# A gather-and-sum graph layer: x rows transposed on TensorE, 66 single rows per step, and steps of the start and the end moved

## The chip, the cores and the metric

The kernel runs on one core of a Trainium2 chip. The metric is the device time of one execution in microseconds; the median of several executions counts.

## The reference

One layer of a graph network with 50,000 nodes of 128 float32 features and 1,650,000 edges, sorted by destination. Each node has an edge to itself.

```
Xs   = x[src]
msg  = where(edge_type == 0, Xs @ W_data.T + b_data, Xs @ W_control.T + b_control)
agg  = segment_sum(msg, dst)
h    = x + relu(agg + x @ W_self.T + b_self)
out  = (h - mean(h)) / sqrt(var(h) + 1e-5)          # per node
```

## The kernel before, in words

The kernel first sums rows of x per destination and per edge type, and multiplies by the weights after that. Edges are cut into blocks that follow each other in the sorted list. A block has Q = 2 steps; a step has R = 12 chunks of 128 edges, F = 42 edges whose rows are found in another way, and S = 64 single edges. So a block covers BE = 24 x 128 + 2 x 42 + 2 x 64 = 3284 edges (lines 35 to 45). There are NBLK = 503 blocks. The first and the last are "plain": chunks only. The last has RCH = 13 chunks.

**Gathers (line 464).** For every chunk GpSimd (POOL) issues one indirect DMA that brings 128 rows of x into a buffer. Six chunks are a pass; a block has four passes; there are SLOTS = 10 buffers of one pass each. TensorE (PE) waits for a pass with a semaphore (line 471), and then multiplies each chunk of rows with a one-hot matrix of 128 x 120 (line 483), which sums the rows by destination (60 columns) and type (two halves).

**Single rows (lines 428 to 443).** For the S single edges of a step, each row of x is loaded with a DMA of its own, half by SP and half by the scalar engine (ACT). Before the DMAs of a step, each of the two loads the byte offsets of its 32 rows from SBUF into registers with one instruction (line 435). The rows are for the block AHEAD = 2 blocks later. PE waits for them at line 449 and adds them with the product of line 489. The offsets are computed by the vector engine (DVE) in `offsets` (line 426).

**The F edges.** DVE finds which of the block's edges to the node itself, for which the node's own row is at hand, can be replaced by these edges, and puts new indices into the gather's list (`fill`, lines 300 to 330), five blocks ahead. What was left out is added back from the transposed rows xT (line 361).

**The window of a block (lines 386 to 396).** A block's sums lie in a window of B = 112 nodes. SP loads the window's first node from SBUF into a register, one block at a time (line 387), then loads the rows of x twice: as they are (xw, 112 x 128, line 393) and transposed (xT, 128 x 112, line 395, from a transposed copy of x in device memory). This is three blocks ahead.

**The layer (lines 514 to 543).** PE adds xT with the self weights, the biases and the two sums with their weights in a PSUM tile po (lines 517, 518, 520). DVE makes h = max(po, 0) + xw (line 525), then the moments (527, 529); ACT takes the root (534); DVE scales (540, 542); SP stores the rows (543).

**The order of the work** is written out by hand in the loop at line 566 for each block and pass, and each engine's queue keeps it. At the head of a block stand the window of block b + 3, then the last sums of the block before; behind the first pass the layer and the moments of the block before, the one-hot matrix for block b + 2 and the single rows of its first step; behind the second pass the root and the counts; behind the third the store, `fill` for b + 5 and the single rows of the second step; behind the fourth the offsets for b + 3.

**The start.** The weights are loaded into two buffers that are freed afterwards and transposed by PE (lines 904 to 911). SP's first load is the index list of block 0 (line 116). POOL makes the number row num (line 120) and the matrix below (133); DVE copies num to PSUM (127).

**The end.** When all blocks are done, DVE and PE work out a flag that tells whether the input breaks an assumption (lines 615 to 640). All engines load the flag (line 919), and branch over a general version that is used only if it is set.

Of the kernel before, what the change touches and what calls it, by code (L numbers as in the profile page):

```python
# [11 lines left out]
F32 = mybir.dt.float32  # L12
# [10 lines left out]
N = 50000  # L23
# [11 lines left out]
W = 60  # L35
# [2 lines left out]
B = 112  # L38
C = R * Q
F = 42  # L40
S = 64
X = Q * S
R1 = R + 1
C1 = Q * R1
# [40 lines left out]
def straight(ctx, tc, c, x, x_t, src_t, dst_t, etype_t, src_f, dst_f, etype_f, src_x, dst_first, first_p, out):  # L85
# [38 lines left out]
    num_ps, rank_no_ps = small[:, :2 * W], small[:, 2 * W:2 * W + F]  # L124
    lists = [small[:, 2 * W + F + i * FILL:][:, :FILL] for i in range(2)]
    sums_at = [small[:Q * F, 2 * W + F + 2 * FILL + i:][:, :1] for i in range(2)]
    nc.vector.tensor_copy(num_ps, num)

    ones_b = keep.tile([P, P], BF16, name="ones_b")
    nc.vector.memset(ones_b, 1.0)  # L130
# [1 line left out]
    below = keep.tile([P, P], BF16, name="below")  # L132
    nc.gpsimd.affine_select(out=below, in_=ones_b, pattern=[[1, P]], compare_op=ALU.is_gt, fill=0.0,
                            base=0, channel_multiplier=-1)
    rank_no = keep.tile([P, F], F32, name="rank_no")
    nc.vector.tensor_scalar(rank_no, num[:, :F], -LOOP, None, op0=ALU.add)
    nc.vector.tensor_copy(rank_no_ps, rank_no)
# [243 lines left out]

    idxs = {0: idx0}
    bys, pcs, zs, pls, bases, ats, ys = {}, {}, {}, {}, {}, {}, {}
    ohs, cnts, accs, xws, xTs, pos, hs, mvs, sds = {}, {}, {}, {}, {}, {}, {}, {}, {}

    def base_of(b):
        return nc.values_load(base_i[0:1, b:b + 1], engines=[SP], min_val=0, max_val=N - B,
                              skip_runtime_bounds_check_because="it was clamped to this")

    def window(b):  # L390
        at = bases[b] = base_of(b)
        xw = stp.tile([B, D], F32, name="xw", bufs=5)
        nc.sync.dma_start(xw, x[bass.ds(at, B), :])
        xT = stp.tile([P, B], F32, name="xT", bufs=5)
        nc.sync.dma_start(xT, x_t[:, bass.ds(at, B)])
        xws[b], xTs[b] = xw, xT

    def onehot(b):
        g, i = divmod(b, GB)
# [13 lines left out]

    ROW_SLOTS = AHEAD + 2
    TURN = S // 2
    LOAD = TURN // 1
    RANGE = dict(min_val=0, max_val=(N - 1) * ROW, skip_runtime_bounds_check_because="where a node's row is")
    x_bytes = x.rearrange("n d -> (n d)").bitcast(U8)[None, :]
    fetched = [[tc.alloc_semaphore(f"fetched{j}_{i}") for i in range(ROW_SLOTS)] for j in range(2)]
# [8 lines left out]
    def single_rows(b, q, part):  # L428

        if q == 0 and part == 0:  # L430
            ys[b] = stp.tile([S, Q, D], F32, name="yx", bufs=ROW_SLOTS)
        both = []
        for j, (eng, dma) in enumerate(((SP, nc.sync), (ACT, nc.scalar))):
            at = j * TURN + part * LOAD
            _, rows = nc.values_load_multi_w_load_instructions(
                ats[b][0:1, q * S + at:q * S + at + LOAD], engines=[eng], **RANGE)
            both.append([(dma, fetched[j][b % ROW_SLOTS], at + k, row) for k, row in enumerate(rows)])
        for pair in zip(*both):
            for dma, sem, k, row in pair:
                copy = dma.dma_start(ys[b][k:k + 1, q, :].bitcast(U8), x_bytes[:, bass.ds(row, ROW)])  # L440
                copy.then_inc(sem, 16)
                tc.no_tile_sem_insts.add(copy.ins.name)
                tc.add_to_no_dep_group(f"single{b}", copy.ins)
# [69 lines left out]

    def layer(b):
        a = sums[b % RING]
        po = ps_o.tile([B, D], F32, name="po")
        nc.tensor.matmul(po, xTs.pop(b), c["wselfT"], start=True, stop=False)  # L517
        nc.tensor.matmul(po, a[0:3, 2, :B], bias, start=False, stop=False)  # L518
        for t in range(2):
            nc.tensor.matmul(po, a[:, t, :B], c["wmsgT"][:, t * D:(t + 1) * D], start=False, stop=t == 1)  # L520
        pos[b] = po

    def moments(b):
        h = stp.tile([B, D], F32, name="h")
        nc.vector.scalar_tensor_tensor(h, pos.pop(b), 0.0, xws.pop(b), op0=ALU.max, op1=ALU.add)  # L525
        st = stp.tile([B, 6], F32, name="st")
        nc.vector.bn_stats(st, h)  # L527
        mv = stp.tile([B, 2], F32, name="mv")
        nc.vector.bn_aggr(mv, st)
        hs[b], mvs[b] = h, mv  # L530
# [6 lines left out]
    def store(b):  # L537
# [4 lines left out]
        nc.vector.tensor_scalar(o, hs.pop(b), mv[:, 0:1], rstd, op0=ALU.subtract, op1=ALU.mult)  # L542
        nc.sync.dma_start(out[bass.ds(bases.pop(b), B), :], o)

    for b in range(1, AHEAD + 1):
        offsets(b)
    columns(0)
# [6 lines left out]
    for b in range(1, RAHEAD):  # L554
        fill(b)
        left_out_columns(b)
        left_out_matrix(b)
        if b < AHEAD:
            onehot(b)
            counts(b)  # L560
            for q in range(Q):
                for part in range(1):
                    single_rows(b, q, part)
        if b == 1:
            clear_sums()
    for b in range(NBLK + 1):
        if b + 3 < NBLK:
            window(b + 3)
        g, i = divmod(b, GB)
        if i == 0 and g + 1 < GROUPS:  # L570
            load_edges(g + 1)
        if i == 3 and g + 1 < GROUPS:
            spread_out(g + 1)
        if i == 4 and g + 1 < GROUPS:
            spread_in(g + 1)
        if b > 0:
            add(b - 1, steps_of(b - 1)[-1])
        if b < NBLK:
            begin_sums(b)
        last = steps_of(b)[-1:]  # L580
        for q, (step, ks) in enumerate(passes_of(b)):
            if ks:
                products(b, step, ks)
            if q == 0 and b > 0:
                layer(b - 1)
            if q == 1:
                left_out_numbers(b + 1)
            if q == 3:
                left_out_columns(b + RAHEAD)
            if ks and step not in last and ks[-1] == chunks_of(b, step)[-1]:  # L590
                add(b, step)
            if q == 0 and b > 0:
                moments(b - 1)
            if q == 0 and b + AHEAD < NBLK:
                onehot(b + AHEAD)
            if q == 1 and b > 0:
                root(b - 1)
            if q == 2 and b > 0:
                store(b - 1)
            if q == 1 and b + AHEAD < NBLK:  # L600
                counts(b + AHEAD)
            if q == 2 and i == 2 and g + 1 < GROUPS:
                columns(g + 1)
            if q == 2:
                left_out_rows(b + 1)
                if b + RAHEAD < NBLK:
                    fill(b + RAHEAD)
            if q == 3:
                left_out_matrix(b + RAHEAD)
                offsets(b + AHEAD + 1)  # L610
            if q % 2 == 0 and not plain(b + AHEAD):
                single_rows(b + AHEAD, q // 2, 0)


    ones = keep.tile([P, 1], F32, name="ones")
    nc.vector.memset(ones, 1.0)
    mm = keep.tile([P, 2], F32, name="mm")
    nc.vector.tensor_reduce(mm[:, 0:1], stats[:, :, 0, :], AX.XY, ALU.min)
    nc.vector.tensor_reduce(mm[:, 1:2], stats[:, :, 1, :], AX.XY, ALU.max)
    bad = keep.tile([P, 3], F32, name="bad")  # L620
    least = keep.tile([P, 1], F32, name="least")
    nc.vector.tensor_reduce(least, loops, AX.X, ALU.min)
    nc.vector.tensor_scalar(bad[:, 2:3], least, float(F), None, op0=ALU.is_lt)
    nc.vector.tensor_scalar(bad[:, 0:1], mm[:, 0:1], 0.0, None, op0=ALU.is_lt)
    nc.vector.tensor_scalar(bad[:, 1:2], mm[:, 1:2], float(W), None, op0=ALU.is_ge)
    gap = keep.tile([1, 3], F32, name="gap")
    nc.vector.tensor_reduce(gap[:, 0:1], shift, AX.X, ALU.min)
    nc.vector.tensor_reduce(gap[:, 1:2], shift, AX.X, ALU.max)
    nc.vector.tensor_scalar(gap[:, 0:1], gap[:, 0:1], 0.0, None, op0=ALU.is_lt)
    nc.vector.tensor_scalar(gap[:, 1:2], gap[:, 1:2], float(B), None, op0=ALU.is_gt)  # L630
    pb = ps_o.tile([B, D], F32, name="po")
    nc.tensor.matmul(pb[:3, 0:1], bad, ones, start=True, stop=True)
    both = keep.tile([3, 1], F32, name="both")
    nc.vector.tensor_copy(both, pb[:3, 0:1])
    pc = ps_o.tile([B, D], F32, name="po")
    nc.tensor.matmul(pc[:1, 0:1], both, ones[:3, 0:1], start=True, stop=True)
    nc.vector.tensor_copy(gap[:, 2:3], pc[:1, 0:1])
    total = keep.tile([1, 1], F32, name="total")
    nc.vector.tensor_reduce(total, gap, AX.X, ALU.add)
    nc.vector.tensor_copy(c["bad"], total)  # L640


def general(ctx, tc, c, x, src, dst, etype, out):
# [221 lines left out]
def gnn_resnorm(  # L865
# [35 lines left out]
    nc.vector.memset(eps, EPS)  # L901
    wmsgT = const.tile([P, 2 * D], F32, name="wmsgT")
    wselfT = const.tile([P, D], F32, name="wselfT")
    with tc.tile_pool(name="wts", bufs=2) as wts, \
            tc.tile_pool(name="wts_ps", bufs=2, space=bass.MemoryType.PSUM) as wts_ps:
        for w, o in ((w_data, wmsgT[:, :D]), (w_ctrl, wmsgT[:, D:]), (w_self, wselfT)):
            w_sb = wts.tile([P, D], F32, name="w_sb")
            nc.scalar.dma_start(w_sb, w)
            pw = wts_ps.tile([P, D], F32, name="pw")
            nc.tensor.transpose(pw, w_sb, ident)  # L910
            nc.scalar.copy(o, pw)
# [63 lines left out]
```

## Time and profile before

| | us |
|---|---|
| timed runs | 24035.24, 24102.25, 24134.87 |
| median | 24102.25 |
| profiled execution, its own time | 15118.55 |
| profiled execution, span | 15116.8 |
| mean granted TensorE clock in it | 0.544 |

The profiled execution is shorter than the timed runs by 8983.70 us. Durations and waits below come from it, since a trace exists for it alone. The page gives busy time and share for each engine, then the chain of work that ended last, then groups of instructions: line, engine, operation, the tiles written and read, the count, busy time and mean duration in ns, and behind the bar the idle time of the engine just before them and what ended it. An engine's name with a q is its queue: control, register loads and the issue of DMAs. "issue" is time in which the engine waited for nothing that the profile shows.

Its DMA queues moved 970.59 MB in 753,407 packets, at 64 GB/s; the 16 DMA engines were busy for 26.4% of the span. Two queues issue the single rows: 32,064 from SP and 32,064 from ACT.

### The profile page before, as it was taken

The page shows a single profiled execution, that of the slowest core. Times are in us where ns is not written, and L with a number is a line of the kernel's source. Part 1 is how long each engine was busy: PE and PEld are TensorE (multiplying, and loading weights), DVE is VectorE, ACT ScalarE, POOL GpSimd, SP SyncE. Part 2 cuts the span into 40 slices and gives each one's busy share as a digit, 9 for nine tenths or more (in the row PEclk, how much of TensorE's full clock was granted, in tenths as well). Part 3 has the DMA queues.
Part 4 walks back from the last instruction along what each step waited for, and adds up shares of the span by engine and source line. Part 5 has one row for each costly group of instructions (what it writes and reads, how often), then busy time and mean ns, then how long its engine had stood idle before and what let it go on. Part 6 is the DMA issues. An engine that isn't in the chain of part 4 may idle for free.

```text
span 15116.8 us, 243274 instructions
## 1 busy us (share of the span) xinstructions
PE 8042.1 (53%) x34836; PEld 6872.7 (45%) x34837; DVE 10626.1 (70%) x13316; ACT 151.7 (1%) x509; POOL 11399.7 (75%) x12071
## 2 busy tenths in 40 slices
PE   3555555555555555555555555555555555555555
PEld 3444444444444444444444444444444444444444
DVE  8776676767767767776676767767777676767765
ACT  0000000000000000000000000000000000000000
POOL 7777777777777777777777777777777777777777
PEclk7555555555555555555555555555555555555555
DMA  2332222222222222222222222222222222222222
GB/s 66 64 65 64 65 65 64 64 65 65 64 65 64 65 64 65 64 65 64 65 64 65 64 65 64 65 64 65 65 64 64 65 65 64 64 65 65 64 65 58
DMA packets 753407, 970.59 MB, mean 64 GB/s; under 512 B 355317, under 2 KB 552100, under 8 KB 751779
## 3 DMA queue, kind: packets, MB, share of 16 engines
q0 software_dynamic: 385968, 791.19, 21.5%
q1 hardware_dynamic: 301244, 146.99, 4.0%
q10 hardware_dynamic: 64566, 16.74, 0.6%
q14 instruction: 1345, 11.01, 0.2%
q8 instruction: 284, 4.65, 0.1%
HBM read 924.76 MB, written 29.02 MB: 63 GB/s over the span
## 4 chain that ended last, share of the span: by engine, by line
POOL 59%; issue 20%; PE 9%; DMA 6%; DVE 4%; ACTq 1%; SPq 0%; POOLq 0%; PEldq 0%; ACT 0%; PEld 0%; DVEq 0%
POOL y L464 59%; DMA y<-in_x,idx 6%; PE acc L483 6%; PE po L520 2%; PE po L518 1%; PE po L517 1%; ACTq L440 1%; DVE cnt L409 0%; DVE by L329 0%; DVE h L525 0%; DVE st L527 0%; DVE m L310 0%; DVE new L313 0%; DVE v_new L317 0%; DVE old L326 0%
## 5 line engine op out<-in xcount | busy, mean ns | idle before, releaser
L464 POOL DMA_INDIRECT y<-in_x,idx x12048 | 11385.9, 945 | 3683.0 <-issue 3573.7
L483 PE MATMUL acc<-oh,y 128*128 128x120 f32 x24122 | 5753.1, 428 | 6277.9 <-PEq L471 6263.0
L483 PEld LDWEIGHTS acc<-oh,y 128*128 128x128 f32 x24122 | 5208.8, 325 | 6688.2 <-PEq L471 6663.4
L409 DVE TENSOR_REDUCE cnt<-oh 128x240 bf16<-128x3120 f32 x503 | 2914.2, 5794 | 0.1
L525 DVE SCALAR_TENSOR_TENSOR h<-po,xw 112x128 f32<-112x128 f32 x503 | 146.7, 292 | 2994.7 <-PE po L520 2937.1
L401 DVE TENSOR_TENSOR oh<-col,small 128x3120 f32<-128x3120 f32 x503 | 1695.9, 3372 | 0.0
L329 DVE TENSOR_REDUCE by<-old 128x84 bf16<-128x1092 f32 x501 | 1066.7, 2129 | 17.4
L499 DVE TENSOR_TENSOR sums<-acc,sums 128x180 f32 x1006 | 347.2, 345 | 960.0 <-PE acc L492 900.9
L489 PE MATMUL acc<-oh,yx 64*128 64x120 f32 x2004 | 769.3, 485 | 7.4 <-PEq L449 7.4
L310 DVE TENSOR_TENSOR m<-rk,small 128x1092 f32<-128x1092 f32 x501 | 647.3, 1292 | 17.1
L313 DVE TENSOR_TENSOR new<-m,small 128x1092 f32<-128x1092 f32 x501 | 647.1, 1292 | 17.1
L317 DVE TENSOR_REDUCE v_new<-new 128x26 f32<-128x1092 f32 x501 | 646.8, 1291 | 17.1
L326 DVE TENSOR_TENSOR old<-m,small 128x1092 f32<-128x1092 f32 x501 | 643.2, 1284 | 0.0
L489 PEld LDWEIGHTS acc<-oh,yx 64*128 64x128 f32 x2004 | 492.5, 303 | 215.9 <-issue 204.6
L520 PE MATMUL po<-wmsgT,sums 128*112 128x128 f32 x2012 | 527.7, 408 | 0.0
L336 PE MATMUL small<-ones_b,by 128*84 128x1 bf16 x501 | 113.0, 225 | 733.2 <-DVE by L329 728.7
L520 PEld LDWEIGHTS po<-wmsgT,sums 128*112 128x112 f32 x2012 | 383.7, 262 | 111.9 <-issue 97.8
L336 PEld LDWEIGHTS <-by 128*84 128x84 bf16 x501 | 73.7, 147 | 791.0 <-DVE by L329 787.1
L518 PE MATMUL po<-bias,sums 3*112 3x128 f32 x1006 | 356.9, 452 | 0.2 <-DVE sums L499 0.2
L517 PE MATMUL po<-wselfT,xT 128*112 128x128 f32 x1006 | 316.9, 419 | 0.0
L512 DVE TENSOR_TENSOR sums<-pl,sums 128x336 f32<-128x336 f32 x501 | 254.3, 508 | 85.0 <-DVE sums L499 83.9
L534 ACT ACTIVATE sd<-mv,eps 112x1 f32<-112x1 f32 x503 | 148.3, 295 | 14831.2 <-PE acc L483 6098.9
(115 smaller groups left out, 3640.2 us busy)
## 6 DMA issues: line engine op xcount, KB each, us to landing
yx<-in_x ACTq DMA_DIRECT2D x32064, 0.5 KB
yx<-in_x SPq DMA_DIRECT2D x32064, 0.5 KB
y<-in_x,idx POOLq DMA_INDIRECT x12048
xw<-in_x SPq DMA_DIRECT2D x503, 56.0 KB
xT<-in_x_t SPq DMA_DIRECT2D x503, 56.0 KB
out<-o SPq DMA_DIRECT2D x503, 56.0 KB
vf_all<-vd SPq DMA_DIRECT2D x51, 420.0 KB
s<-in_src_t SPq DMA_DIRECT2D x51, 130.0 KB
```

Source lines behind the costliest of these rows:

```text
L310: nc.vector.tensor_tensor(m, rk_g[g][:, i, :, None].to_broadcast([P, C1, F]), rank_no_ps[:, None, :].to_broadcast([P, C1, F]), op=ALU.is_e ...
L313: nc.vector.tensor_tensor(new.rearrange("p (q r) f -> p q r f", r=R1), m.rearrange("p (q r) f -> p q r f", r=R1), vf.rearrange("p (q f) -> ...
L317: nc.vector.tensor_reduce(v, new, AX.X, ALU.add)
L326: nc.vector.tensor_tensor(old, m, cb[:, :, None].to_broadcast([P, C1, F]), op=ALU.mult)
L329: nc.vector.tensor_reduce(by, old.rearrange("p (q r) f -> p q f r", r=R1), AX.X, ALU.add)
L401: nc.vector.tensor_tensor(oh, col_g[g][:, i, :, None].to_broadcast([P, C1, 2 * W]), num_ps[:, None, :].to_broadcast([P, C1, 2 * W]), op=AL ...
L409: nc.vector.tensor_reduce(cnt, ohs[b].rearrange("p (q r) w -> p q w r", r=R1), AX.X, ALU.add)
L464: copy = nc.gpsimd.indirect_dma_start(out=y[:r, k % PASS, :], out_offset=None, in_=x, in_offset=bass.IndirectOffsetOnAxis(ap=idxs[b][:r, c ...
L483: nc.tensor.matmul(acc[:, :2, :].rearrange("p t w -> p (t w)"), y[:r, k % PASS, :], ohs[b][:r, column(k), :], start=k == of_step[0], stop= ...
L489: nc.tensor.matmul(acc[:, :2, :].rearrange("p t w -> p (t w)"), ys[b][:, q, :], ohs[b][:S, q * R1 + R, :], start=False, stop=True)
L518: nc.tensor.matmul(po, a[0:3, 2, :B], bias, start=False, stop=False)
L520: nc.tensor.matmul(po, a[:, t, :B], c["wmsgT"][:, t * D:(t + 1) * D], start=False, stop=t == 1)
```

## The change

- S goes from 64 to 66. A block covers 3288 edges, and there are 502 blocks; the last has 23 chunks, the last chunk 112 edges.
- The single rows of a step are loaded in two parts of 17 and 16 rows for each of SP and ACT, behind every pass instead of every other one. Each part has its own load of offsets.
- xw is no longer loaded. PE transposes xT into a second half of the PSUM tile po, DVE copies that to h, and then adds max(po, 0) to it.
- The bases of the windows are loaded for five blocks with one instruction.
- The weights have a buffer each, which is not freed. The copy of num to PSUM stands behind the making of below.
- The flag is worked out before the last block's gathers instead of after everything; its code is otherwise the same.

```
-S = 64
+S = 66
...
-    nc.vector.tensor_copy(num_ps, num)
...
     nc.gpsimd.affine_select(out=below, in_=ones_b, pattern=[[1, P]], compare_op=ALU.is_gt, fill=0.0,
                             base=0, channel_multiplier=-1)
+    nc.vector.tensor_copy(num_ps, num)
...
+    BASES = 5
     def window(b):
-        at = bases[b] = base_of(b)
-        xw = stp.tile([B, D], F32, name="xw", bufs=5)
-        nc.sync.dma_start(xw, x[bass.ds(at, B), :])
+        if b % BASES == 0:
+            n = min(BASES, NBLK - b)
+            _, regs = nc.values_load_multi_w_load_instructions(
+                base_i[0:1, b:b + n], engines=[SP], min_val=0, max_val=N - B,
+                skip_runtime_bounds_check_because="it was clamped to this")
+            bases.update({b + i: at for i, at in enumerate(regs)})
+        at = bases[b]
...
-    LOAD = TURN // 1
+    LOAD = -(-TURN // 2)
...
             at = j * TURN + part * LOAD
+            n = min(LOAD, (j + 1) * TURN - at)
             _, rows = nc.values_load_multi_w_load_instructions(
-                ats[b][0:1, q * S + at:q * S + at + LOAD], engines=[eng], **RANGE)
+                ats[b][0:1, q * S + at:q * S + at + n], engines=[eng], **RANGE)
...
     def layer(b):
         a = sums[b % RING]
-        po = ps_o.tile([B, D], F32, name="po")
-        nc.tensor.matmul(po, xTs.pop(b), c["wselfT"], start=True, stop=False)
+        both = ps_o.tile([B, 2, D], F32, name="po")
+        po, xT = both[:, 0, :], xTs.pop(b)
+        nc.tensor.transpose(both[:, 1, :], xT, c["ident"])
+        nc.tensor.matmul(po, xT, c["wselfT"], start=True, stop=False)
...
     def moments(b):
         h = stp.tile([B, D], F32, name="h")
-        nc.vector.scalar_tensor_tensor(h, pos.pop(b), 0.0, xws.pop(b), op0=ALU.max, op1=ALU.add)
+        po = pos.pop(b)
+        nc.vector.tensor_copy(h, po[:, 1, :])
+        nc.vector.scalar_tensor_tensor(h, po[:, 0, :], 0.0, h, op0=ALU.max, op1=ALU.add)
...
     for b in range(NBLK + 1):
+        if b == NBLK - 1:
+            find_bad()
...
-            if q % 2 == 0 and not plain(b + AHEAD):
-                single_rows(b + AHEAD, q // 2, 0)
+            if not plain(b + AHEAD):
+                single_rows(b + AHEAD, q // 2, q % 2)
...
-        for w, o in ((w_data, wmsgT[:, :D]), (w_ctrl, wmsgT[:, D:]), (w_self, wselfT)):
-            w_sb = wts.tile([P, D], F32, name="w_sb")
+        for i, (w, o) in enumerate(((w_data, wmsgT[:, :D]), (w_ctrl, wmsgT[:, D:]), (w_self, wselfT))):
+            w_sb = w_all[:, i, :]
```

## The prediction

> **What bounds the kernel now.** I read the page first: the busy shares, then the chain that ended last, then the costliest groups.
>
> ```profile
> PE 8042.1 (53%) x34836; PEld 6872.7 (45%) x34837; DVE 10626.1 (70%) x13316; ACT 151.7 (1%) x509; POOL 11399.7 (75%) x12071
> ...
> POOL 59%; issue 20%; PE 9%; DMA 6%; DVE 4%; ACTq 1%; SPq 0%; POOLq 0%; PEldq 0%; ACT 0%; PEld 0%; DVEq 0%
> ...
> L464 POOL DMA_INDIRECT y<-in_x,idx x12048 | 11385.9, 945 | 3683.0 <-issue 3573.7
> ```
>
> No engine looks full, but POOL is: of its 3683.0 us of idle time, 3573.7 us is "issue", time in which it waited for nothing shown. A gather is 0.945 us of work and about 0.30 us between two of them. The view by stages confirms that nothing interrupts this (columns: stretch, length, then PE, PEld, DVE, ACT, POOL busy with counts, clock, DMA share, GB/s):
>
> ```profile
> 3000.00:6000.00 3000.00, 1614.23 (x6930) 1377.82 (x6930) 2112.13 (x2641) 29.47 (x100) 2267.24 (x2401) 0.54 0.26 64
> 6000.00:9000.00 3000.00, 1616.61 (x6930) 1379.32 (x6930) 2112.09 (x2638) 29.48 (x100) 2267.62 (x2400) 0.53 0.26 64
> ```
>
> 2400 gathers in 3000 us, so 1.250 us each; a block has 24, so 30.0 us. The kernel has 502x24 + 13 = 12,061 gathers, and 12,061 x 1.250 = 15,076 us of a 15,116.8 us span. The gather count is the time. PE and DVE have slack: DVE is busy 2112/100 = 21.1 us of each 30.0 us block.
>
> The next in line are SP and ACT, which issue the single rows. For the lines that load row offsets (L435) and window bases (L387), the duration columns are min/median/max in ns:
>
> ```profile
> L435 ACTq TENSOR_LOAD <-at_x x1002: 2131/2154/2428, 20.8 to 15003.1; - x167
> L435 SPq TENSOR_LOAD <-at_x x1002: 1866/2077/2373, 32.9 to 15014.4; - x167
> ...
> L387 SPq TENSOR_LOAD <-base_i x503: 280/542/772, 28.5 to 14997.2; - x168
> ```
>
> In the timeline 32 rows take 10.3 us on either queue, 0.322 us a row. ACT per block: 2x10.3 + 2x2.15 + 0.3 (its square root) = 25.2 us, 4.8 idle. SP: 2x10.3 + 2x2.08 + 0.54 + about 0.5 each for xw and xT with their register work + 0.5 for the store = 26.8 us. SP's own list of waits gives what remains:
>
> ```profile
> SPq L543 <- DVE o L542: 726.7, 337, 27.5
> SPq L435 <- DVE sums L512: 127.0, 48, 16.7
> SPq L543 <- DVE h_loop L255: 125.7, 46, 3.7
> SPq L543 <- DVE pl L361: 112.0, 48, 17.0
> ```
>
> With the smaller entries it adds to about 1300 us, 2.6 us per block: SP works 27.4 of 30.0 us, by these waits. It is the resource that this change can overfill.
>
> **The start and the end.** The timeline at the start and near the end:
>
> ```profile
> 6.23 0.42 SPq L116 DMA_DIRECT2D idx<-in_src_t  x1
> ...
> 8.38 1.15 POOL L464 DMA_INDIRECT y<-in_x,idx  x1 [0.66 <-DMA idx<-in_src_t]
> ...
> 41.73 0.94 POOL L464 DMA_INDIRECT y<-in_x,idx  x1 [1.68 <-DVE idx L321]
> ```
>
> ```profile
> 15091.92 1.00 POOL L464 DMA_INDIRECT y<-in_x,s  x1 [0.30 <-issue]
> ...
> 15101.20 0.35 DVE L542 TENSOR_SCALAR o<-h,mv,rstd 112x128 f32<-112x128 f32 x1
> ...
> 15104.34 0.14 DVE L640 CAST bad<-total 1x1 int32<-1x1 f32 x1
> ```
>
> SP issues nothing before 6.23 us, when the weights' buffers are freed. After the last gather 25 us remain, 2.9 us of them for the flag.
>
> **What the Trainium skill says.** "SBUF — State Buffer", Who interferes with whom: a VectorE copy that uses both SBUF port pairs locks GpSimd out of writing descriptors, which would hit gathers. The trace agrees at the start, where gathers beside large conversions take up to 1.64 us; in steady state the mean is 0.945. "VectorE: DVE Perf Modes", the section Why `tensor_tensor` can't do 2×_2P or 4×, says an operand in PSUM excludes that mode, and the new copy reads PSUM. "Runtime: NRT & Kernel Launch", Instruction fetch mechanics, gives about 200 ns per register load even in bulk; the trace disagrees: 2154/32 = 67 ns. "DMA: Bandwidth & Descriptors", Issuing engines are not separate DMA queues: all issuers share the 16 DMA engines, and issuing elsewhere saves only sequencer time. The trace fits: DMA is 26% busy.
>
> **The change part by part**, against the profiled execution (15,118.55 us: span 15,116.8 plus 1.75 around it).
>
> 1. *66 rows.* A block covers 24x128 + 84 + 132 = 3288 edges, not 3284. There are then 502 blocks, and the last holds 2928 edges, 23 chunks. Gathers: 501x24 + 23 = 12,047, 14 fewer: 14 x 1.250 = -17.5 us, on the path.
> 2. *Issue of the rows.* Each queue gets 2 rows more a block: +0.64 us. Loads of 32 registers become 17 and 16. From the one-register load (0.54 us on SP, L387; ACT's one-register load of the flag took 0.46) and the 32-register one, SP's slope is (2.077-0.542)/31 = 0.050 us, so 17 registers cost 1.34 and 16 cost 1.29; four loads are 5.26 against 4.15: +1.1 us on SP, likewise +1.0 on ACT. The bounds: at least nothing, if load cost were purely per register; at most +4.15, if it were per load. I take +1.1. Behind these on SP are the store and the next window. SP's order stays (window, first step's rows, store, second step's rows), and the rows are issued two blocks before PE uses them. On ACT the second part of the first step now follows the square root (L534) instead of preceding it, so that comes some 5 us earlier (16 rows x 0.322); DVE waited for it 14.7 us in all, so nothing is gained.
> 3. *xw's load gone, bases five at a time.* SP: -0.50 and -(0.54 - 0.75/5) = -0.39 us. SP's net is +0.64+1.1-0.89 = +0.85: 28.25 of 30.0 us. ACT's is +1.65: 26.9. Both stay under POOL, so nothing on the path; the cover is 1.75 us a block on SP, and each microsecond beyond it costs 500 us in all. The 28.8 MB not read relieve nothing that POOL waits for.
> 4. *Transpose.* By the nearest row (the weights' transposes, 0.448 us, load 0.18), +0.6 us of PE a block, ahead of the layer. PE idles before its gathered rows 6263 us in all, 12 us a block: hidden. Were it not, the matmuls start 0.6 us later and the ten-pass gather buffer still covers it.
> 5. *Copy of the transpose.* Nearest: h from PSUM, 128 columns, 0.292 us. DVE goes from 21.1 to 21.4 of 30.0: hidden. If it did lock POOL, 0.29x501 = +145 us; POOL's constant pitch beside the copies at L307 and L308 and the PSUM operand speak against it: 0.
> 6. *Start.* With its own weight buffer SP need not wait for 6.23 us, and can start near 0.9, where ACT's first load is. All of SP's first loads move together, the one that DVE's chain waits for (first_i) too, so the wait at 41.73 moves with them. -5.3 us; bounds 0 (another wait holds SP) and -5.3.
> 7. *The flag before the last block.* It takes 2.9 us off the end; PE's branch (3.97 us, L921) can start when PE is done, which may give 2 more. Its two PSUM tiles, its two small matmuls and about 3 us of DVE work now stand ahead of the last block's sums and products on DVE and PE, while POOL still gathers; DVE's 8.6 free us a block cover it. No DMA moves with it. The copy of num moves behind one POOL select at the start; POOL then reaches its gathers without waiting for the copy's PSUM. The last pass has 5 chunks, not 1: +1.0 us. Net -2 to -4: -3.
>
> Sum: -17.5 - 5.3 - 3 = **-26 us**, 15,092 for the profiled execution.
>
> **From there to the median.** The timed runs have a median of 24,102.25 us, 8984 us above the profiled execution, 59%. No view shows those 8984 us. If they are a constant, the change brings -26; if each gather is longer in proportion (24,102/12,061 = 2.0 us), -28-8 = -36. I take the middle: **24,071 us**, -0.13%. What is measurable here is about 0.5%, so this is "no change".
>
> **Rivals.**
> *SP becomes the pace (slower).* For it: 28.25 of 30.0 us, and four loads that each stop the queue. It decides when a load costs 1.75/4 = 0.44 us more than the 1.3 taken. At 2.08, a cost per load, SP needs 27.4+0.64+4.15-0.89 = 31.3 us, +1.3x501 = +650 us, less the block saved (30): 24,720. Nearly the same comes out if in the longer timed runs SP already is the pace: 24,102 x 28.25/27.4 x 502/503 = 24,800. I take 24,750. Against it: one-register loads take 0.54, so most of the cost is per register.
> *The transfers count (faster).* If the unseen 8984 us come from DMA traffic, 28.8 of 970.6 MB gone are 3.0% of it: -267 - 26, so 23,810. For it: xw is 56,336 of 753,407 packets. Against it: DMA engines are 26% busy, and POOL waited for a gather buffer (for PE's products, L483) only 11.7 us.
> *The change has no effect at all:* another wait holds the start and SP's time shifts; 24,085 with the gathers alone. This lies in my own case.
>
> **Numbers.** My case (with the no-effect one) 0.67, transfers 0.18, SP 0.15. Its own range, with both readings of the median and run-to-run spread (24,035 to 24,135), is 23,990 to 24,170. The range for 8 in 10 reaches down to the transfers case and up to a slightly overfilled SP (0.4 us a block, +200): 23,800 to 24,270. Faster by over 0.5%: 0.18; within: 0.67; slower: 0.15.
>
> **What would show it.** Gathers 12,047 at an unchanged 1.250 us; the first one near 3 us; L435's successors near 1.3 us; SP's waits about 1.6 us a block; DVE copy near 0.29. Wrong if POOL waits for PE at its buffers, PE for the row semaphore, or the gather lengthens beside the new copy.

## The result, and the profile after

| | before, us | after, us | ratio (95% interval) |
|---|---|---|---|
| median of 5 runs | 24103.84 | 26185.91 | 1.0864 (1.0842 to 1.0885) |
| lowest and highest | 24035.24, 24134.87 | 26136.66, 26211.52 | |
| profiled execution, own time | 15118.55 | 26136.66 | |
| its span | 15116.8 | 26134.6 | |

The kernel became 8.6% slower, where the prediction was no change. The two profiled executions can't be subtracted: that of after is one of the timed runs, that of before is 8985 us shorter than the median of its timed runs. The experiments point to the chip: on four of the five that they ran on, before takes 15,119 to 15,120 us; on the fifth it takes 23,761, and in the result's timed runs 24,104. By their times, before's profile is from a chip of the first kind and after's from one of the second. Each chip was used on one occasion only, so what is called a kind of chip here may also be something else that differed between the occasions. Every ratio below is against before on the same chip.

The page of after, the same parts as before's: the chain by engine and by line, then groups.

```profile
SPq 63%; issue 28%; DVE 5%; PE 2%; DMA 1%; ACTq 1%; another core or an unknown queue 0%; DVEq 0%; PEldq 0%; ACT 0%; PEld 0%
SPq L443 41%; SPq L438 19%; DVE cnt L411 2%; SPq L550 1%; DVE oh L403 1%; DMA yx<-in_x 1%; PE acc L486 1%; SPq L397 1%; PE acc L492 1%; DVE by L329 0%; ACTq L443 0%; DVE m L310 0%; DVE new L313 0%; PE po L525 0%; DVE v_new L317 0%
...
L467 POOL DMA_INDIRECT y<-in_x,idx x12024 | 11383.3, 947 | 14624.7 <-PE acc L486 9913.7
...
L492 PE MATMUL acc<-oh,yx 66*128 66x120 f32 x2000 | 599.3, 393 | 13722.7 <-PEq L452 13722.7
```

Read them from the end. The chain, once 59% POOL, now is SP's queue: 41% issue of rows (L443), 19% loads of their offsets (L438). PE stood 13,722.7 us before the product of the single rows (L492), for their semaphore (L452); POOL then stood 9913.7 us for PE to free gather buffers (L486). A gather is as long as ever, 947 ns, but comes less often, 1391 in 3000 us instead of 2400:

```profile
3000.00:6000.00 3000.00, 808.46 (x4080) 749.91 (x4080) 1251.63 (x1594) 16.80 (x57) 1316.37 (x1391) 0.57 0.14 36
```

The loads of offsets, for which the prediction wanted 1.3 us (min/median/max in ns):

```profile
L438 ACTq TENSOR_LOAD <-at_x x2000: 4/3656/4267, 16.7 to 26033.4; - x182
L438 SPq TENSOR_LOAD <-at_x x2000: 4/3081/3812, 31.8 to 26100.8; - x182
```

A load of half as many registers takes longer than the 2154 ns that 32 took. All of them added up are 6129 us on ACT and 5494 us on SP, 12.2 and 10.9 us a block, where two loads of 32 had cost 4.3 and 4.15. (The shortest, 4 ns, show that single durations of this trace can't be trusted; the last section returns to it.) The first gather starts at 3.25 us (8.38 before), and the copy of the transpose takes 292 ns, both as predicted.

### The profile page after: what moved, and what is told of

The parts are those of the page before. It is cut to its first block, busy times and chain, and to the rows that moved or that the text cites. A ratio compares the mean times of both kernels' runs of the same rounds, so it can differ in the third digit from the quotient of the medians.

```text
span 26134.6 us, 248180 instructions
## 1 busy us (share of the span) xinstructions
PE 6930.0 (27%) x35290; PEld 6431.9 (25%) x35291; DVE 10826.1 (41%) x13794; ACT 151.1 (1%) x508; POOL 11406.6 (44%) x12057
## 4 chain that ended last, share of the span: by engine, by line
SPq 63%; issue 28%; DVE 5%; PE 2%; DMA 1%; ACTq 1%; another core or an unknown queue 0%; DVEq 0%; PEldq 0%; ACT 0%; PEld 0%
SPq L443 41%; SPq L438 19%; DVE cnt L411 2%; SPq L550 1%; DVE oh L403 1%; DMA yx<-in_x 1%; PE acc L486 1%; SPq L397 1%; PE acc L492 1%; DVE by L329 0%; ACTq L443 0%; DVE m L310 0%; DVE new L313 0%; PE po L525 0%; DVE v_new L317 0%
## 5 line engine op out<-in xcount | busy, mean ns | idle before, releaser
L467 POOL DMA_INDIRECT y<-in_x,idx x12024 | 11383.3, 947 | 14624.7 <-PE acc L486 9913.7
L486 PE MATMUL acc<-oh,y 128*128 128x120 f32 x24094 | 5069.7, 396 | 7.8 <-issue 7.8
L486 PEld LDWEIGHTS acc<-oh,y 128*128 128x128 f32 x24094 | 4833.7, 306 | 7.9 <-issue 7.7
L492 PE MATMUL acc<-oh,yx 66*128 66x120 f32 x2000 | 599.3, 393 | 13722.7 <-PEq L452 13722.7
L492 PEld LDWEIGHTS acc<-oh,yx 66*128 66x128 f32 x2000 | 424.0, 264 | 13845.4 <-PEq L452 13845.0
L531 DVE COPY h<-po 112x128 f32<-112x128 f32 x502 | 146.5, 292 | 1687.0 <-PE po L525 1645.6
L310 DVE TENSOR_TENSOR m<-rk,small 128x1092 f32<-128x1092 f32 x500 | 646.0, 1292 | 17.5 <-issue 0.5
```

Source lines behind the costliest of these rows:

```text
L310: nc.vector.tensor_tensor(m, rk_g[g][:, i, :, None].to_broadcast([P, C1, F]), rank_no_ps[:, None, :].to_broadcast([P, C1, F]), op=ALU.is_e ...
L467: copy = nc.gpsimd.indirect_dma_start(out=y[:r, k % PASS, :], out_offset=None, in_=x, in_offset=bass.IndirectOffsetOnAxis(ap=idxs[b][:r, c ...
L486: nc.tensor.matmul(acc[:, :2, :].rearrange("p t w -> p (t w)"), y[:r, k % PASS, :], ohs[b][:r, column(k), :], start=k == of_step[0], stop= ...
L492: nc.tensor.matmul(acc[:, :2, :].rearrange("p t w -> p (t w)"), ys[b][:, q, :], ohs[b][:S, q * R1 + R, :], start=False, stop=True)
```

## The experiments

**One part at a time.** One chip; before takes 15,118.57 us there. `base` is before once more, to get a trace of the execution of 24,100 us.

> The kernel before, unchanged, to get a trace of it at the speed of its timed runs. The trace shown before had a span of 15,117 us, the timed runs a median of 24,104 us. Theory Q (SP and ACT pace the timed runs: each issues single rows at well over 0.322 us a row, and POOL waits): span near 24,100 us, rows at about 0.45 to 0.6 us, offset loads above 2.2 us, POOL waiting for PE, PE for the single rows. Rival G (every gather is longer in the timed runs): POOL busy without waits, a pitch of 2.0 us, rows at 0.322 us. If the trace shows 15,100 us again, neither is told apart.

It took 15,118.71 us with a span of 15,117.0. It tells nothing of the longer executions. `base_2`, on the last of the five chips (before: 15,119.52 us), was a second try:

> The kernel before, for its trace on a chip where it takes about 24,000 us (of the chips so far one in four, and that of the result). There: rows at 0.45 us or more on both queues, in stalls of about 0.7 us that hit both queues at once, as in the trace of the change; SP or ACT leads the chain that ended last; gathers at 1.25 us with waits between them. If the chip gives 15,120 us, this stays open.

It took 15,120.1. There is no trace of before on a chip of the second kind.

`split64` is before with its loads in two parts, 16 and 16, and 64 rows:

```
-    LOAD = TURN // 1
+    LOAD = -(-TURN // 2)
...
-            if q % 2 == 0 and not plain(b + AHEAD):
-                single_rows(b + AHEAD, q // 2, 0)
+            if not plain(b + AHEAD):
+                single_rows(b + AHEAD, q // 2, q % 2)
```

> Only the loading of the single rows in two parts (16 and 16 of each queue, behind every pass), with 64 rows and xw as before. Theory L (the offset loads pay per instruction while the other queue issues rows; four of them a block instead of two): most of the 8.6% appears here, ratio 1.05 to 1.09. Rival R (the two additional rows per queue and block cost it): ratio within 1% of 1.00.

15,119.13 us, ratio 1.000 (0.9991 to 1.0009). The loads:

```profile
L436 ACTq TENSOR_LOAD <-at_x x2004: 1187/1297/1527, 20.7 to 15016.3; - x183
L436 SPq TENSOR_LOAD <-at_x x2004: 973/1227/1658, 32.7 to 15021.2; - x183
```

Here are the prediction's 1.29 us for 16 registers. Twice the loads at this price fit beside POOL; splitting is not the cause on such a chip.

`noxw` is before with xw replaced by the transpose and the copy, nothing else:

```
-        xw = stp.tile([B, D], F32, name="xw", bufs=5)
-        nc.sync.dma_start(xw, x[bass.ds(at, B), :])
...
+        nc.tensor.transpose(both[:, 1, :], xT, c["ident"])
...
+        nc.vector.tensor_copy(h, po[:, 1, :])
+        nc.vector.scalar_tensor_tensor(h, po[:, 0, :], 0.0, h, op0=ALU.max, op1=ALU.add)
```

> Only xw replaced by the transpose on PE and the copy on DVE; 64 rows in one part, one base load per block. Theory L: SP saves about 0.5 to 1 us of a 48 us block, ratio 0.98 to 1.00. Rival T (the transpose or the copy lengthens the path from the sums to the next block, or slows the gathers): ratio 1.02 or more.

15,116.08 us, 0.9998 (0.9989 to 1.0007). `noxw_2`, on the last chip, repeats it:

> Only xw replaced by the transpose. Where the kernel before takes about 24,000 us and SP paces: SP issues about 0.5 us less of 47 us a block, ratio 0.985 to 1.00. Where it takes 15,120: 1.000.

15,116.37 us, 0.9998 again. Copy and transpose are hidden, and the 28.8 MB saved bring nothing on these chips.

`after_s64` is the changed kernel with `S = 64`, so with all of the change but the row count.

> The changed kernel with 64 rows per step instead of 66 (two parts of 16). Theory L: 1.03 to 1.07, that is nearly all of the loss stays and only about 2 rows in 66 of a block (1.4 us of 52) are saved. Rival R: ratio at or below 1.01.

15,105.7 us, 0.9992 (0.9983 to 1.0). Repeated on the last chip as `after_s64_2`:

> The changed kernel with 64 rows per step, where all loads are aligned. Where the kernel before takes about 24,000 us: from 66 to 68 aligned rows the time rose by 1.9%, so 64 should give 24,195/23,761 less 1.9%, a ratio of 0.995 to 1.005, if the four loads and the missing xw weigh nothing. Where it takes 15,120: 0.999.

15,106.9 us, 0.9991. So all of the change but the 66 rows brings 12 to 13 us, and on such a chip nothing but the 66 is left that could make the kernel slower.

**Is it the 66?** Another chip; before 15,118.68. `after_again` is the changed kernel, unedited; `s66split` is before with `S = 66` and the split of `split64`, xw kept.

> The changed kernel, unchanged, beside the kernel before on a chip where that one takes 15,119 us if it is the same chip as in the last call. Theory P (POOL paces both kernels there; the 8.6% comes only where SP and ACT issue more slowly than 0.322 us a row): 15,085 to 15,105 us, ratio 0.998 to 0.999, gathers at 1.25 us. Rival K (66 rows overfill SP whatever the chip): over 20,000 us, rows at 0.55 us or more, as in the trace of the change.

> Only the 66 rows, in two parts of 17 and 16; xw is still loaded, bases one at a time, start and end as before. Theory P: 15,095 to 15,115 us where the kernel before takes 15,119 (14 gathers fewer, 17.5 us; the last pass 1 us longer). Rival K: as slow as the changed kernel or slower, since SP has 0.9 us a block more to do than there.

18,146.18 us, 1.2004 (1.1984 to 1.2024), and 18,566.36 us, 1.2283 (1.2263 to 1.2304). Both theories missed: P said no loss, and K said over 20,000 us. `after_2`, on the last chip, gave 18,141.97, 1.2001:

> The changed kernel once more. Where the kernel before takes about 24,000 us: ratio 1.07 to 1.10. Where it takes 15,120: 1.20.

So 66 rows cost a fifth even where before takes 15,119 us. `s66split` is the slower of the two; it still loads xw and one base per block, and by its page SP is most of the chain (SPq 54%), where the changed kernel has ACT. Page and loads of `after_again`, then single loads of one block (the count 1, one duration three times, and the start):

```profile
ACTq 80%; issue 13%; DVE 5%; PE 2%; ACT 1%; DVEq 0%; DMA 0%; SPq 0%
...
L438 ACTq TENSOR_LOAD <-at_x x2000: 1203/3834/4136, 16.7 to 18098.5; - x182
L438 SPq TENSOR_LOAD <-at_x x2000: 1196/3533/3832, 26.7 to 18092.8; - x182
```

```profile
L438 ACTq TENSOR_LOAD <-at_x x1: 3663/3663/3663, 9007.9 to 9007.9; - x1
...
L438 ACTq TENSOR_LOAD <-at_x x1: 3930/3930/3930, 9017.0 to 9017.0; - x1
...
L438 ACTq TENSOR_LOAD <-at_x x1: 1366/1366/1366, 9026.8 to 9026.8; - x1
...
L438 ACTq TENSOR_LOAD <-at_x x1: 3908/3908/3908, 9033.7 to 9033.7; - x1
```

Three long, one short, whatever the count of registers (16, 17, 16, 17); so it is in every block. What differs is where each list begins in the tile of offsets. Step q, queue j, part p begins at byte 4 x (66q + 33j + 17p). ACT's four lists begin at 132, 200, 396 and 464, SP's at 0, 68, 264 and 332. Of these only 0 and 464 are multiples of 16, and only the load from 464 is short on ACT; on SP three loads take 3521 to 3676 ns and the one from byte 0 takes 1377, though it has 17 registers. With 64 rows every list begins at a multiple of 64. ACT's block is full: in the timeline its 66 rows reach over 32.1 us, with three of these loads (9.2 us) between them, so 0.347 us a row; with the fourth load, 3.7, and the root, 0.3, that is 36.1 us, and 18,131.6/502 = 36.1. ACT sets the pace.

That made a new theory: a load from a start that isn't a multiple of 16 bytes fetches register by register.

**The starts alone.** A third chip; before 15,120.18. `aligned66` is the changed kernel with a tile that gives each list of a queue 36 words, and parts of 20 and 13. The starts are then 0, 80, 144, 224, ..., multiples of 16, not all of 32:

```
-    LOAD = -(-TURN // 2)
+    LOAD = 20
...
-            ats[b] = stp.tile([1, X], I32, name="at_x", bufs=AHEAD + 2)
+            ats[b] = stp.tile([1, Q, 2, 36], I32, name="at_x", bufs=AHEAD + 2)
...
-                ats[b][0:1, q * S + at:q * S + at + n], engines=[eng], **RANGE)
+                ats[b][0:1, q, j, part * LOAD:part * LOAD + n], engines=[eng], **RANGE)
```

> The changed kernel with nothing different but where the row offsets lie: each queue's 33 offsets of a step start at a multiple of 36 words, and the parts are 20 and 13, so that every load starts at a multiple of 16 bytes. Theory M (a load whose first word is not at a multiple of 16 bytes fetches word by word, some 0.21 us a register; an aligned one four words at a time): loads of 1.1 to 1.6 us throughout, 15,085 to 15,105 us where the kernel before takes 15,119, ratio 0.998 to 0.999. Rival N (the number of rows or of loads overfills the queues): as slow as the changed kernel on that chip (ratio 1.2).

15,088.23 us, 0.9979 (0.997 to 0.9987):

```profile
L440 ACTq TENSOR_LOAD <-at_x x2000: 1178/1429/1771, 16.6 to 14985.5; - x182
L440 SPq TENSOR_LOAD <-at_x x2000: 1124/1262/1597, 26.9 to 14990.6; - x182
...
L469 POOL DMA_INDIRECT y<-in_x,idx x12024 | 11363.8, 945 | 3677.0 <-issue 3530.0
...
3000.00:6000.00 3000.00, 1536.61 (x7048) 1379.29 (x7049) 2144.28 (x2740) 29.48 (x100) 2267.55 (x2400) 0.56 0.28 63
```

All loads are short, POOL's idle time is "issue" again, and 2400 gathers run in 3000 us. Moving the lists takes 3058 us away from the changed kernel (18,146.18 us on the previous chip).

Not every load is at a multiple of 16, as the expectation has it: the bases of the windows still begin at bytes 0, 20, 40, 60 and so on, so only every fourth of these loads of five registers does (min/median/max in ns):

```profile
L391 SPq TENSOR_LOAD <-base_i x101: 742/1329/1489, 24.4 to 14936.2; - x101
```

Every fourth of them takes about 0.78 us, the three between about 1.33. That is the same pattern in another list, and with one such load in five blocks it costs little.

`shift64` does the opposite: before, with 64 rows and one load of 32 registers each, but SP's lists start 8 and ACT's 4 bytes past a multiple of 16.

```
+            ats[b] = stp.tile([1, Q, 2, 44], I32, name="at_x", bufs=AHEAD + 2)
...
-                ats[b][0:1, q * S + at:q * S + at + LOAD], engines=[eng], **RANGE)
+                ats[b][0:1, q, j, 2 - j:2 - j + LOAD], engines=[eng], **RANGE)
```

> The kernel before with nothing different but where its row offsets lie: SP's 32 of a step start 8 bytes past a multiple of 16, ACT's 4 bytes past one. Same rows, same number of loads. Theory M: loads of 32 registers take about 7 us instead of 2.15 (32 x 0.21 + 0.45) on both queues, so ACT needs 25.2 + 2x5 = 35 us and SP 27.4 + 10 = 37 us a block instead of the 30.0 that POOL needs: 17,600 to 18,900 us. If 8 bytes are enough, only ACT's loads are long. Rival N: 15,119 us, loads at 2.15.

18,735.29 us, 1.2391 (1.2366 to 1.2416):

```profile
L439 ACTq TENSOR_LOAD <-at_x x1002: 6953/7026/7244, 21.6 to 18606.1; - x167
L439 SPq TENSOR_LOAD <-at_x x1002: 6471/6682/6859, 33.7 to 18661.0; - x167
```

7026/32 = 220 ns a register, against 67 before. Nothing but the starts has changed, with the tile that holds the lists and a second DVE instruction to fill it, and it costs 24%. Eight bytes of alignment aren't enough. The time per register fits the theory; that the registers are fetched one by one is inferred from such times, no view shows it.

`after72` asks how many rows fit when the lists are aligned: 72 rows, parts of 20 and 16, 501 blocks, 12,002 gathers (and a guard for a group of blocks that has become empty).

> The changed kernel with 72 rows per step, where the parts (20 and 16 of each queue) start at multiples of 16 bytes without padding: 501 blocks, 12,002 gathers, 59 fewer than before. Theory M: -59 x 1.25 = -74 us and 8 us at start and end: 15,035 to 15,060 us, if the queues keep below 30.0 us a block (72 x 0.33 + 4 x 1.4 = 29.4 on either, with little left; SP adds xT and the store, about 1.2: 30.6, then some 15,300). Rival N: above 18,000 us.

15,870.11 us, 1.0496 (1.0478 to 1.0513). Both times of theory M were missed, and so was rival N's. The loads stayed short (1426 and 1264 ns), but the chain by engine is

```profile
SPq 40%; DVE 21%; DMA 16%; issue 14%; PE 6%; ACTq 4%; DVEq 0%; PEldq 0%; ACT 0%
```

SP is full here without any long load. In the trace it issues 6813 rows in 3000 us, 31.7 us a block; less 0.7 of waits and 6.5 of other work (four loads 5.28 and a fifth of a base load 0.24, both as means; xT and store 0.5 each, by the prediction's prices) a row costs an estimated 0.34 us rather than 0.322. The room lies between 66 and 72 rows.

**On a chip of the second kind.** Before takes 23,761.08 us there. `aligned66_2` is `aligned66` again, `aligned68` the same with `S = 68` (parts 20 and 14, also 502 blocks).

> The aligned offsets with 66 rows once more. If the kernel before takes 24,100 us on this chip, as in the timed runs of the result, theory M says that alignment is all of the 8.6% and more: ratio at or below 1.00 (in the trace of the change the queues' loads take 12.2 and 10.9 us a block, aligned ones 5.5). If a ratio near 1.08 remains there, something else makes the change slow on that chip. If the kernel before takes 15,120 us, the ratio is 0.998 again.

> The same with 68 rows per step (parts of 20 and 14, aligned): 12,032 gathers. If the queues still have room (in the run with 66 rows they are idle for about 1 us a block, and 2 rows on each are 0.65 to 0.9 us): 15,065 to 15,080 us. If the step from 66 to 72 (15,870) grows evenly past the point where SP is full: up to 15,350.

24,194.64 us, 1.0178 (1.0161 to 1.0195), and 24,662.6 us, 1.0382 (1.0364 to 1.0399). Theory M's ratio at or below 1.00 was missed; the times for 68 rows were meant for a chip of the first kind. The loads are short on this chip too (medians 1311 and 1224 ns in `aligned66_2`), and yet SP is the pace; chain of `aligned66_2`:

```profile
SPq 57%; issue 35%; DVE 4%; PE 2%; DMA 1%; ACTq 0%; another core or an unknown queue 0%; PEldq 0%; PEld 0%; DVEq 0%; ACT 0%
SPq L445 47%; SPq L440 7%; DVE cnt L411 2%; SPq L552 1%; DMA yx<-in_x 1%; SPq L397 1%; PE acc L488 1%; PE acc L494 0%; DVE by L329 0%; ACTq L445 0%; DVE m L310 0%; DVE new L313 0%; DVE v_new L317 0%; DVE old L326 0%; SPq L164 0%
```

A block takes 23,761.08/503 = 47.24 us before, 48.20 with 66 and 49.13 with 68 rows: two more rows per queue cost 0.96 and 0.93 us, so about 0.47 us for each row added, with what changes beside it: in the first step four loads for two, no xw and fewer loads of bases; in the second a register more in two of the four loads, about 0.2 us each. Both steps cost nearly the same. That is what a queue that already sets the pace would do.

## Why the prediction was wrong

**Step 2 failed, the issue of the rows.** It put a load of 17 or 16 registers at 1.34 and 1.29 us, "four loads are 5.26 against 4.15: +1.1 us on SP". Four loads took 12.2 us on SP and 12.9 on ACT (means over the blocks of `after_again`), +8.0 and +8.6. The bound, "at most +4.15, if it were per load", didn't hold it, since both ends assumed that only count and number of loads matter. The start of the list matters: `aligned66` and `shift64` show it in both directions. At aligned starts the step's prices were about right: 1.30 us for 16 registers on ACT, and in `aligned66`, with loads of 20 and 13, four on SP take 5.29 us. Step 3's price for the bases, 0.75 us, holds for one load in four; the others take 1.33.

**What the skill said was half of it.** The Trainium skill, "Runtime: NRT & Kernel Launch", Instruction fetch mechanics, gives about 200 ns per register even in bulk; by the page's list of terms it means loads from device memory, where the lists here lie in SBUF. The prediction set it aside for the 67 ns of the trace. The trace of before was right for its own lists, and lists that begin off multiples of 16 bytes cost 220 ns a register, close to the page's figure; that both have one cause is not shown. Two prices so far apart asked for the condition that divides them; the trace of before, where each list starts at a multiple of 128, couldn't show it.

**The rival "SP becomes the pace"** had the mechanism. It decided "when a load costs 0.44 us more than the 1.3 taken"; three of four cost 2.2 to 2.6 us more. Its price (+650 us) was too small, and in the changed kernel on a chip of the first kind ACT, which has the longer loads, fills first (ACTq 80% of the chain).

**From there to the median** failed too. The 8984 us were held to be a constant or in proportion to the gathers. On the one chip of the second kind with experiments, the chain of `aligned66_2` is SP's issue, and added rows cost what they would on a queue that is the pace. The rival's second reading, "if in the longer timed runs SP already is the pace", fits this. The result's 1.0864 then divides into 1.0178 for the change with aligned lists and 1.0864/1.0178 = 1.067 for the starts of the lists. The two ratios are from two chips, and the changed kernel itself was not run on that one, so this split is an estimate. In after's trace too, three of four loads are long on either queue, by the medians.

**What was right** can be read from `aligned66`, against before's profile; all three terms are on the timelines:

| term | predicted, us | measured, us |
|---|---|---|
| start: first gather, 8.38 to 3.21 | -5.3 | -5.2 |
| gathers: first to last, 15,083.5 to 15,067.5 | -17.5 | -16.1 |
| end: last gather to the end, 24.9 to 15.7 | -3 | -9.1 |
| sum, the difference of the spans | -26 | -30.4 |

The end brought three times the forecast. The times come from these lines: the last store of before, then the first gather and the end of `aligned66`:

```profile
15101.57 0.32 SPq L543 DMA_DIRECT2D out<-o  x1
...
3.21 1.12 POOL L469 DMA_INDIRECT y<-in_x,idx  x1 [1.09 <-DMA idx<-in_src_t]
...
15070.66 0.93 POOL L469 DMA_INDIRECT y<-in_x,s  x1 [0.30 <-issue]
...
15078.36 0.29 DVE L533 COPY h<-po 112x128 f32<-112x128 f32 x1 [2.16 <-PE po L527]
...
15080.51 0.32 SPq L552 DMA_DIRECT2D out<-o  x1
```

From the last store's issue to the end of the span (15,086.4) are 5.9 us; before it was 15.2 us from 15,101.57, with 2.9 us of flag in it. So some 6 us of what followed the flag, its load and the branches, had also been on the path; the prediction counted 2 of them. The gathers' pitch stayed at 1.250 us, so the new copy doesn't hold POOL up. "SBUF — State Buffer", Who interferes with whom, had let one expect this for a copy outside the modes that use both port pairs; that an operand in PSUM excludes them is stated by "VectorE: DVE Perf Modes" in its section Why PSUM operands drop a tier. SP's waits add up to 661 us, 1.3 us a block, where 1.6 were expected.

**Open.** Why an added row costs about 0.47 us on a chip of the second kind isn't settled, nor whether the chip itself makes the difference; the last section shows what the trace has of it. That SP is the pace of before as well is inferred from the two equal steps and from the changed kernels' chains, not shown.

**The better version** is `aligned66`: -0.21% where before takes 15,120 us. On the chip of 23,761 us it is 1.8% slower than before, so it isn't better everywhere; there 64 rows, or fewer, would have to be tried, which wasn't done.

## What to carry to other kernels

When a size changes, work out the byte at which each list that is loaded into registers begins: here the loads stayed cheap with starts at multiples of 16 bytes, and padding the tile was all it took to get them. Price an instruction's new form by what could differ in it, its address as well as its count, and let the bounds reach to the dearest price that any source gives. When the profiled execution is far below the timed runs, it may show another limit than the one that is timed: name which resource would be next there, and weigh added work on it as if it were already the pace.

## What the runs showed of the hardware

- One load of registers from SBUF into ACT, on chips of the first kind: 1.30 us for 16 and 2.15 for 32 registers from starts at multiples of 16 bytes; 3.66 for 16, 3.93 for 17 and 7.03 for 32 from starts 8, 12 and 4 bytes past one.
- From starts at multiples of 16 the durations on SP look as if four registers were fetched at once and each that is left over by itself: 1.23 us for 13 (`aligned66`) and for 16 (`split64`), 1.42 for 14 (`aligned68`), 1.39 for 17 (`after_again`) and for 20 (`aligned66`), each the median at one place of the block. This is inferred, not shown.
- In the traces of the second kind SP and ACT stall while they issue rows. The chain of waits of after, one stretch (start, length, what):

```profile
12020.55 0.27 SPq L443
...
12020.91 0.69 issue
...
12021.63 0.70 issue
...
12022.33 0.70 issue
...
12023.75 0.70 SPq L443
12024.45 0.72 issue
```

The usual step of 0.27 gives way to steps of 0.70 us, both inside an instruction (SPq L443) and between two of them (issue). In before's trace the longest issue of a row is 0.71 us, on SP; the median is 0.23. The stalls fall on register moves too, which need no DMA: for the moves of L443, in after and then in `after_again`, min/median/max in ns are

```profile
L443 SPq MOVE yx<-in_x x33000: 1/29/1465, 31.9 to 26109.5; - x199
...
L443 SPq MOVE yx<-in_x x33000: 29/29/40, 28.0 to 18101.5; - x199
```

So it is the queue that stops, not the row's DMA alone, while a gather keeps its 947 ns. What the queues wait for, no view shows.
